# LayerNorm statistics joined on GpSimd in an attention and ternary feed-forward layer

## The chip, the cores and the metric

The kernel runs on one core of a Trainium2 chip. The time is the device time of one execution in microseconds (us); the time before is the median of three runs. The engines are called as the profile calls them: PE (TensorE matrix products; PEld its weight loads), DVE (VectorE), ACT (ScalarE), POOL (GpSimd) and SP (SyncE, which only issues DMAs here).

## The reference, cut to what matters

The input x has 8 batches of 1024 tokens with 256 features. Four LayerNorms over the 256 features stand in the layer:

```python
x = x + layernorm(attention(layernorm(x), Wq, Wk, Wv, Wo))
x = x + layernorm(ternary_ffn(layernorm(x), weight, alpha, bias))

def layernorm(x, eps=1e-05):
    m = mean(x, axis=-1); v = var(x, axis=-1)
    return (x - m) / sqrt(v + eps)
```

The attention has 16 heads of 16 features on 4 key and value heads, with rotary positions, softmax over 1024 keys, and an output product. The feed-forward part is one 256x256 product with weights in {-1, 0, 1}, scaled by alpha, plus a bias.

## The kernel before

**Units and blocks.** The work is cut into 16 units of 512 tokens (four tiles of 128 tokens on the 128 partitions; two units are one batch). Each unit has four blocks of attention, one for each of four groups of heads: 64 blocks, each some 25 us long. In a block PE makes the scores twice: once with queries on the partitions (tile sm, L600), from which DVE takes the maxima of the rows (mx, L625), and once with keys on the partitions, shifted by those maxima (se, L673), from which ACT takes the exponentials (e, L694). PE then sums them with the values (av, L714). The maxima go back into the stacked queries through PE (L648), ACT (L650), DVE (ml, L657) and two DMAs by SP (L664). Each block's maxima are made ahead of its exponentials.

**What runs between the blocks.** Class Project makes a later unit's queries, keys and values: LayerNorm of x in two halves p = 0 and 1 (begin: statistics, xn, its split into a high and a low part xs), transposes pt_xt, products, rotation of the queries (rotate, L315 to L317) and of the keys (kt), their split (split, L157 and L162, tiles hlq and ks), and stores to DRAM (dq, dk), from where DMAs stack them into q_st and k_st. Class Tail takes an earlier unit's attention output to the end: fetch and scale, the output product pa (attn), stats_a with x1 = x + layernorm, stats_x with the second LayerNorm xn and its split hl, transposes pt_ot (x, L267), the feed-forward product (ffn, with the bias added on POOL at L853), stats_f and the output (end). Tables such as P_PARTS and T_PARTS give the step of the schedule at which each part stands; there are 32 steps to a unit. Unit 0's tail and the first projects have tables of their own (T_FIRST, P_FIRST, P_SECOND). Units 12 to 14 use another form of the tail, which transposes xn itself (xw).

**Order.** PE's, DVE's and ACT's instructions run in the order in which the program writes them. POOL's do so only at the start and in the last unit's end; in the long middle part the framework's scheduler chooses POOL's order, and SP's, from its own estimates:

```python
with tc.manual_schedule(engines={E.PE, E.DVE, E.Activation}):
    while s < 4 * NSTEP:
        s = window(s)
```

Each engine works its own queue in order and waits for the others by semaphores.

**Statistics.** ln_stats (L231 to L244) makes bn_stats for each of one or two tiles on DVE (L237; six numbers for each token: count, mean and sum of squared deviations of the even columns, and the same of the odd ones), then bn_aggr on DVE (L239; mean and variance, tile mv), then three small steps on POOL: variance plus epsilon (L241), the power -0.5 (L242) and the negative mean (L243), into tile lnsc. ln_apply (L253) uses them on POOL, or on DVE for parts of the start and of the last unit. There are 134 calls: eight at the start (units 0, 1 and 2), 26 in the projects from unit 3 on, 90 in the tails of units 0 to 14, and twelve in the last unit's, which go one tile at a time, the first tile on POOL and the other three on DVE. The small tiles have four buffers each.

Of the kernel before, what the change touches and what calls it, by code (L numbers as in the profile page):

```python
# [8 lines left out]
F32 = mybir.dt.float32  # L9
F32R = mybir.dt.float32r  # L10
AF = mybir.ActivationFunctionType
ALU = mybir.AluOpType
# [4 lines left out]
P = 128  # L17
# [6 lines left out]
EPS = 1e-5  # L24
# [4 lines left out]
def kernel(  # L29
# [29 lines left out]
    nc = tc.nc  # L59
    B, S, D = x.shape  # L60
# [14 lines left out]
    small = ctx.enter_context(tc.tile_pool(name="small", bufs=4))  # L75
# [10 lines left out]
    def load_x(u, tag, bufs):  # L86
        b, half = divmod(u, UPB)
        t = xp.tile([P, UT, D], F32, tag=tag, name=f"{tag}_{u}", bufs=bufs)
        src = x[b, half * UQ : (half + 1) * UQ, :].rearrange("(t p) d -> p t d", p=P)
        for ts in (slice(0, 2), slice(2, 4)) if u == 0 else (slice(0, 4),):  # L90
            nc.sync.dma_start(out=t[:, ts, :], in_=src[:, ts, :])
        return t

    x_sb = {0: load_x(0, "x", 2)}
# [4 lines left out]
    mhalf = const.tile([P, 2], F32, name="mhalf")  # L99
# [128 lines left out]
        nc.scalar.copy(wt, pt)  # L228


    def ln_stats(src):  # L231

        n = src.shape[1]
        mv = small.tile([P, 2, 2], F32, tag="mv", name="mv")[:, :n]
        st = small.tile([P, 2, 6], F32, tag="bnst", name="bnst")
        for t in range(n):
            nc.vector.bn_stats(st[:, t, :], src[:, t, :])  # L237
        for t in range(n):
            nc.vector.bn_aggr(mv[:, t, :], st[:, t, :])  # L239
        sc = small.tile([P, 2, 2], F32, tag="lnsc", name="lnsc")[:, :, :n]  # L240
        nc.gpsimd.tensor_scalar(sc[:, 1, :], mv[:, :, 1], EPS, 1.0, ALU.add, ALU.mult)  # L241
        nc.gpsimd.tensor_tensor(sc[:, 1, :], sc[:, 1, :], mhalf[:, :n], ALU.pow)  # L242
        nc.gpsimd.tensor_scalar(sc[:, 0, :], mv[:, :, 0], -1.0, 0.0, ALU.mult, ALU.add)  # L243
        return mv, sc  # L244

    def ln_apply(eng, dst, src, stats):
        mv, sc = stats
        for t in range(src.shape[1]):
            if eng is nc.scalar:
                eng.activation(dst[:, t, :], src[:, t, :], AF.Identity, bias=sc[:, 0, t : t + 1])  # L250
                eng.mul(dst[:, t, :], dst[:, t, :], sc[:, 1, t : t + 1])
                continue
            eng.tensor_scalar(  # L253
                dst[:, t, :],
                src[:, t, :],
                sc[:, 0, t : t + 1] if eng is nc.gpsimd else mv[:, t, 0:1],
                sc[:, 1, t : t + 1],
                ALU.add if eng is nc.gpsimd else ALU.subtract,
                ALU.mult,
            )  # L260
# [62 lines left out]
    class Project:  # L323
# [19 lines left out]
                    for p in range(2)  # L343
                ]

        def stats(self, p):
            self.sc[p] = ln_stats(x_sb[self.u][:, 2 * p : 2 * p + 2, :])

        def norm(self, p, eng=None):
            src = x_sb[self.u][:, 2 * p : 2 * p + 2, :]  # L350
# [6 lines left out]
            split_lo(eng or self.eng, self.xs[p][1], self.xn[p], self.xs[p][0])  # L357

        def begin(self, p):
            self.stats(p)  # L360
            self.norm(p)
            self.hi(p)
            self.lo(p)
# [374 lines left out]
    class Tail:  # L738
# [88 lines left out]
            ln_apply(self.eng(p), self.on[p], self.x1[p], self.sc[p])  # L827

        def stats_a(self, p):
            self.sc[p] = ln_stats(self.a[p])  # L830
            self.add(p)

        def stats_x(self, p):
            self.sc[p] = ln_stats(self.x1[p])
            self.norm(p)
            if not NU - 4 <= self.u < NU - 1:
                self.split(p)

        def stats_f(self, p):
            self.sc[p] = ln_stats(self.a[p])  # L840
            self.end(p)

        def ffn(self, p):
# [482 lines left out]
```

## Time and profile before

| What | Value |
|---|---|
| Median of three runs | 1629.83 us (1627.93 to 1637.51) |
| The profiled execution | 1631.22 us, span 1629.4 us, mean granted PE clock 0.993 |
| Busy PE / DVE / ACT / POOL | 1578.1 / 1398.3 / 1270.4 / 833.2 us |
| bn_aggr on DVE, two-tile and one-tile calls (L239) | 256 instructions, 38.6 us |
| Power on POOL, 128x2 (L242) | 122 instructions, 85.7 us |
| Idle POOL ahead of L241 | 337.8 us in all |

The profile is of one execution. Busy is the time in which an engine works on an instruction; the span runs from the first to the last instruction, and the execution's own time is some 1.8 us longer. A group of instructions is told by line, engine, operation, tiles written and read with their shapes, and count; then busy time in us, mean ns of one, and the idle time of the engine just before them with what ended most of it. A line of a timeline has start and duration in us, engine, line, operation and tiles, and in brackets the idle time before it. "x2" after it means two such instructions in a row.

### The profile page before, as it was taken

The numbers are of one execution on the slowest core, as the hardware profiler recorded it, in microseconds if no ns is written. First come the engines' busy times: TensorE is split into PE (matmuls) and PEld (weight loads), VectorE is DVE, ScalarE is ACT, GpSimd is POOL, SyncE is SP. The second block draws the span as 40 slices with busy tenths as digits, with TensorE's granted clock in tenths as the row PEclk, the third lists the DMA queues.
The fourth block names the chain that finished last, engine by engine and source line by source line (L and its number), as shares of the span: only waits on it lengthen the run. The fifth ranks groups of instructions, "written<-read, shape, count | busy, mean of one in ns | idle before, by whom it ended". The sixth has DMA issues, their size and how long they took to land.

```text
span 1629.4 us, 37176 instructions
## 1 busy us (share of the span) xinstructions
PE 1578.1 (97%) x14698; PEld 816.7 (50%) x14698; DVE 1398.3 (86%) x2050; ACT 1270.4 (78%) x2473; POOL 833.2 (51%) x1239
## 2 busy tenths in 40 slices
PE   7999999999999999999999999999999999999997
PEld 5544454554545545454544545455454554444444
DVE  7878888889898888989889898988989888999964
ACT  4667878788787887878788787887878787787784
POOL 5542357374654647455364845546474552333354
PEclk8999999999999999999999999999999999999999
DMA  4151516124141422514133161413314151131100
GB/s 140 53 83 49 106 53 113 62 67 112 57 108 47 88 71 60 125 47 104 61 79 80 57 128 38 103 56 82 80 57 97 47 105 46 43 74 34 42 15 27
DMA packets 86078, 117.98 MB, mean 72 GB/s; under 512 B 12088, under 2 KB 50808, under 8 KB 85752
## 3 DMA queue, kind: packets, MB, share of 16 engines
q1 hardware_dynamic: 85904, 115.60, 29.7%
q8 instruction: 116, 1.90, 0.5%
q14 instruction: 58, 0.48, 0.1%
HBM read 68.65 MB, written 45.88 MB: 70 GB/s over the span
## 4 chain that ended last, share of the span: by engine, by line
PE 81%; DVE 10%; POOL 3%; ACT 2%; issue 1%; DMA 1%; SPq 0%; POOLq 0%; ACTq 0%; DVEq 0%
PE av L714 29%; PE se L673 28%; PE sm L600 9%; DVE mx L625 8%; PE pa L301 3%; PE pq L301 3%; PE pf L301 2%; ACT e L694 2%; PE pt_xt L267 2%; PE pt_ot L267 1%; PE pkv L301 1%; PE pm L648 1%; DVE bnst L237 1%; POOL lnsc L242 0%; POOL xn L253 0%
## 5 line engine op out<-in xcount | busy, mean ns | idle before, releaser
L625 DVE TENSOR_REDUCE mx<-sm 128x2 f32<-128x1024 f32 (+1 forms) x1305 | 1205.1, 972 | 184.4 <-PE sm L600 164.7
L694 ACT ACTIVATE e<-se 128x512 f32<-128x512 f32 x1996 | 1056.9, 603 | 221.6 <-PE sm L600 176.2
L600 PE MATMUL sm<-k_st,q_st 64*128 64x512 f32 x2048 | 747.3, 449 | 7.9 <-DVE mx L625 4.6
L673 PE MATMUL se<-q_st,k_st 64*128 64x512 f32 x2048 | 705.9, 441 | 17.1 <-ACT e L694 14.6
L714 PE MATMUL av<-e,v_aug 128*32 128x256 f32 (+3 forms) x8600 | 605.7, 378 | 0.0
L673 PEld LDWEIGHTS se<-q_st,k_st 64*128 64x128 f32 x2048 | 325.1, 185 | 392.6 <-ACT e L694 303.6
L600 PEld LDWEIGHTS sm<-k_st,q_st 64*128 64x128 f32 x2048 | 325.7, 185 | 68.8 <-DVE mx L625 46.0
L714 PEld LDWEIGHTS av<-e,v_aug 128*32 128x32 f32 x8600 | 193.9, 109 | 213.0 <-issue 148.7
L241 POOL TENSOR_SCALAR lnsc<-mv 128x2 f32<-128x2 f32 (+1 forms) x134 | 25.6, 191 | 337.8 <-DVE mv L239 331.2
L788 POOL TENSOR_TENSOR xn<-xn,a 128x512 f32<-128x512 f32 x30 | 38.4, 1281 | 130.0 <-DMA a<-d_rec 104.5
L242 POOL TENSOR_TENSOR lnsc<-lnsc,mhalf 128x2 f32<-128x2 f32 (+1 forms) x134 | 92.2, 689 | 0.9
L157 POOL TENSOR_SCALAR xs<-xn 128x512 fp32r<-128x512 f32 x27 | 17.1, 634 | 128.3 <-DMA dq<-hlq 127.0
L162 POOL TENSOR_TENSOR hl<-xn,hl 128x512 fp32r<-128x512 f32 x54 | 68.7, 1284 | 0.1
L853 POOL TENSOR_TENSOR a<-a,bias_bc 128x512 f32<-128x512 f32 x30 | 38.4, 1280 | 53.7 <-ACT a L852 53.7
L253 POOL TENSOR_SCALAR xn<-x,lnsc 128x256 f32<-128x256 f32 x116 | 64.2, 560 | 2.3
L301 PE MATMUL pa<-woh,hl 128*128 128x256 f32 x240 | 46.2, 295 | 1.1 <-ACT e L694 1.1
L315 POOL TENSOR_TENSOR t<-q_rot,sin_q_sb 128x512 f32<-128x512 f32 x31 | 39.6, 1279 | 12.8 <-ACT q_rot L457 12.7
L237 DVE BATCH_NORM_STATS2 bnst<-x 128x6 f32<-128x256 f32 x124 | 45.9, 412 | 0.0
L301 PE MATMUL pq<-xt,wqkvh 128*128 128x256 f32 x256 | 45.0, 299 | 0.5 <-ACT e L694 0.5
L237 DVE BATCH_NORM_STATS2 bnst<-a 128x6 f32<-128x256 f32 x120 | 44.5, 413 | 0.1
L162 POOL TENSOR_TENSOR hlq<-q_rot,hlq 128x512 fp32r<-128x512 f32 x31 | 39.8, 1284 | 4.8 <-ACT hlq L159 4.5
L457 ACT COPY q_rot<-pq 128x512 f32<-128x512 f32 x32 | 18.7, 585 | 29.5 <-PE pq L301 29.5
(164 smaller groups left out, 1329.7 us busy)
## 6 DMA issues: line engine op xcount, KB each, us to landing
q_st<-dq SPq DMA_DIRECT2D x90, 256.0 KB
dq<-hlq SPq DMA_DIRECT2D x60, 256.0 KB
d_av<-avsb SPq DMA_DIRECT2D x60, 256.0 KB
x<-in_L_attn_x SPq DMA_DIRECT2D x15, 512.0 KB
xn<-d_av SPq DMA_DIRECT2D x30, 256.0 KB
a<-d_rec SPq DMA_DIRECT2D x30, 256.0 KB
xr<-in_L_attn_x SPq DMA_DIRECT2D x15, 512.0 KB
out_x<-a SPq DMA_DIRECT2D x30, 256.0 KB
```

Of the source, the lines that this page charges most:

```text
L162: eng.tensor_tensor(lo, src, hi.bitcast(F32), ALU.subtract)
L237: nc.vector.bn_stats(st[:, t, :], src[:, t, :])
L242: nc.gpsimd.tensor_tensor(sc[:, 1, :], sc[:, 1, :], mhalf[:, :n], ALU.pow)
L253: eng.tensor_scalar(dst[:, t, :], src[:, t, :], sc[:, 0, t : t + 1] if eng is nc.gpsimd else mv[:, t, 0:1], sc[:, 1, t : t + 1], ALU.add i ...
L267: nc.tensor.transpose(pt[:, c, t * P : (t + 1) * P], src[:, t, c * P : (c + 1) * P], ident_r)
L301: nc.tensor.matmul(out, chunk(left[i], c), chunk(right[j], c), start=(k == 0), stop=(k == len(steps) - 1),)
L315: eng.tensor_tensor(dst, x, table.unsqueeze(1).to_broadcast(list(x.shape)), ALU.mult)
L600: scores = nc.tensor.matmul(sm[0][:, part, :], queries[rows], k_st[(u // UPB) % 3][rows, r2, ch * 512 : (ch + 1) * 512], start=True, stop= ...
L625: early[0] = nc.vector.tensor_reduce(mx[i][:, a, head_and_tile(i, r2, t), lo:n], sm[0][:, lo:n, :], AX.X, ALU.max).ins
L673: nc.tensor.matmul(sc if len(queries.shape) == 2 else sc.rearrange("p (j t) -> p j t", j=G), k_st[(i // G // UPB) % 3][rows, r2, kt * P : ...
L694: nc.scalar.activation(e, sc, AF.Exp, scale=1.0 / D**0.5)
L714: nc.tensor.matmul(av_ps[0][32 * r : 32 * r + 32, lo:hi], va[:, kt, r, :], es[i * NK + kt, r // 2, r % 2][:, lo:hi], start=(kt == 0 and lo ...
```

## The change

A function join_stats is added. Where ln_stats is called with joined_by = nc.gpsimd, DVE makes only bn_stats, and POOL makes mean and variance out of the halves itself, for one or two tiles at once: the negative mean is -0.5 times the sum of the two means; the sums of squares are added and divided by 256, with epsilon; the square of (even mean + negative mean) is added; then comes the power. That is five tensor_tensor, two tensor_scalar and the power, eight instructions in place of POOL's three and DVE's one or two bn_aggr. It holds for the projects' begin (units 3 to 15) and for every tail part whose engine is POOL: units 0 to 14, and the first tile of the last unit. The statistics of units 0 to 2 at the start and of the last unit's other tiles stay as they were.

```diff
-    def ln_stats(src):
+    def join_stats(neg_mean, rstd, st):
+
+        eng, (m0, m1), (s0, s1) = nc.gpsimd, (st[:, 1, i] for i in range(2)), (
+            st[:, 2, i] for i in range(2)
+        )
+        eng.tensor_tensor(neg_mean, m0, m1, ALU.add)
+        eng.tensor_scalar(neg_mean, neg_mean, -0.5, 0.0, ALU.mult, ALU.add)
+        eng.tensor_tensor(s0, s0, s1, ALU.add)
+        eng.tensor_scalar(s0, s0, 1.0 / D, EPS, ALU.mult, ALU.add)
+        eng.tensor_tensor(m0, m0, neg_mean, ALU.add)
+        eng.tensor_tensor(m0, m0, m0, ALU.mult)
+        eng.tensor_tensor(rstd, s0, m0, ALU.add)
+        eng.tensor_tensor(rstd, rstd, mhalf[:, : rstd.shape[1]], ALU.pow)
+
+    def ln_stats(src, joined_by=None):
 
         n = src.shape[1]
-        mv = small.tile([P, 2, 2], F32, tag="mv", name="mv")[:, :n]
         st = small.tile([P, 2, 6], F32, tag="bnst", name="bnst")
         for t in range(n):
             nc.vector.bn_stats(st[:, t, :], src[:, t, :])
+        sc = small.tile([P, 2, 2], F32, tag="lnsc", name="lnsc")[:, :, :n]
+        if joined_by is nc.gpsimd:
+            join_stats(sc[:, 0, :], sc[:, 1, :], st[:, :n].rearrange("p t (i k) -> p k i t", i=2))
+            return None, sc
+        mv = small.tile([P, 2, 2], F32, tag="mv", name="mv")[:, :n]
         for t in range(n):
             nc.vector.bn_aggr(mv[:, t, :], st[:, t, :])
-        sc = small.tile([P, 2, 2], F32, tag="lnsc", name="lnsc")[:, :, :n]
...
-        def stats(self, p):
-            self.sc[p] = ln_stats(x_sb[self.u][:, 2 * p : 2 * p + 2, :])
+        def stats(self, p, joined_by=None):
+            self.sc[p] = ln_stats(x_sb[self.u][:, 2 * p : 2 * p + 2, :], joined_by)
...
         def begin(self, p):
-            self.stats(p)
+            self.stats(p, nc.gpsimd)
...
         def stats_a(self, p):
-            self.sc[p] = ln_stats(self.a[p])
+            self.sc[p] = ln_stats(self.a[p], self.eng(p))
...
         def stats_x(self, p):
-            self.sc[p] = ln_stats(self.x1[p])
+            self.sc[p] = ln_stats(self.x1[p], self.eng(p))
...
         def stats_f(self, p):
-            self.sc[p] = ln_stats(self.a[p])
+            self.sc[p] = ln_stats(self.a[p], self.eng(p))
```

## The prediction

> **What bounds the kernel now.** I read the page first, then the busy time by stages, the chain of work that ended last, the groups of instructions by shape, and the timelines of POOL and PE around the first unit's tail.
>
> ```profile
> PE 1578.1 (97%) x14698; PEld 816.7 (50%) x14698; DVE 1398.3 (86%) x2050; ACT 1270.4 (78%) x2473; POOL 833.2 (51%) x1239
> ...
> PE 81%; DVE 10%; POOL 3%; ACT 2%; issue 1%; DMA 1%; SPq 0%; POOLq 0%; ACTq 0%; DVEq 0%
> ```
>
> PE is busy 97% of the span and carries 81% of the chain; DVE carries 10%. So a shorter DVE pays only in the places where DVE is on that chain. By stages (columns: PE, PEld, DVE, ACT and POOL busy with their counts, PE clock, DMA share, GB/s):
>
> ```profile
> 200.00:300.00 100.00, 97.81 (x954) 50.82 (x954) 86.57 (x131) 79.30 (x154) 56.79 (x82) 1.00 0.39 89
> 900.00:1000.00 100.00, 98.51 (x958) 51.22 (x952) 88.49 (x130) 80.86 (x158) 54.19 (x80) 1.00 0.33 78
> 1400.00:1500.00 100.00, 97.84 (x930) 46.73 (x928) 91.68 (x132) 80.36 (x157) 34.56 (x53) 1.00 0.26 56
> ```
>
> Up to about 1300 us PE hardly pauses. There the chain by stretches of 100 us gives DVE 3.6% (the score maxima alone, no statistics). From 1300 us on, where no projections are left, DVE rises to 14 to 23% of it.
>
> **What is removed from DVE.** 119 of the 134 statistics lose their bn_aggr: 116 with two tiles and 3 with one, 235 instructions. PE's, ACT's and DVE's order is written by hand and otherwise stays.
>
> ```profile
> L239 DVE BATCH_NORM_AGGREGATE mv<-bnst 128x2 f32<-128x6 f32 x256 | 38.6, 173 | 0.4
> L241 POOL TENSOR_SCALAR lnsc<-mv 128x2 f32<-128x2 f32 x122 | 23.3, 191 | 318.5 <-DVE mv L239 312.4
> L242 POOL TENSOR_TENSOR lnsc<-lnsc,mhalf 128x2 f32<-128x2 f32 x122 | 85.7, 702 | 0.5
> L316 POOL TENSOR_TENSOR q_rot<-q_rot,t 128x256 f32<-128x256 f32 x31 | 23.1, 745 | 0.5
> L316 POOL TENSOR_TENSOR k_rot<-k_rot,t2k 128x128 f32<-128x128 f32 x14 | 6.4, 457 | 1.0
> ```
>
> 235 x 0.173 = 40.7 us less DVE work. On the chain stand only nine pairs or singles of L239 between 1300 and 1580 us, eight with 0.22 and one with 0.18 us (the pairs overlap with their neighbours): **-1.9 us**. Its bounds are 0 and all 16 statistics of that stretch at 2 x 0.173, -5.5 us.
>
> **What is added to POOL.** A join is eight instructions, two tensor_scalar, five small tensor_tensor and the power, in place of two tensor_scalar and the power. A two-column tensor_tensor without a power isn't in the trace. From the rows with 256 and 128 columns, (745 - 457) / 128 = 2.25 ns a column, so two columns end near 0.17 us; I take 0.19, the tensor_scalar's row. The lower bound is 0.10 (the 128x2 memset of L100 took 99 ns), the upper one 0.70, the power, which is the same instruction in the same shape. 119 x 5 x 0.19 = 113 us more POOL work, 833 to 946 of 1629: still far from full, so only queueing counts. A statistic alone in an idle POOL is ready 0.95 us later, less the 0.35 that DVE gives back.
>
> [...] The row first: L241 to L243 starts 0.27 us apart where its span is 0.19. [...]
>
> **Steady units (1 to 11).** PE first needs POOL's result in the transposes pt_ot of the tail. The trace has the first half of hl ready 3.7 to 5.3 us before its transpose for p = 0 (unit 1: written 343.77, used 347.52) and 5.6 us or more before for p = 1. POOL's queue isn't ordered by hand after the start. In the built kernel the join's steps stand between the query's rotation and split, and the low half of that split (1.28 us) now goes ahead of hl. So hl is late by 1.28 + 0.95 = 2.2 us, some 2.5 with waits: inside every slack. x1 is 0.7 us late where DVE comes 8 us after. The next unit's x is waited for by POOL itself behind a DMA of 11 to 13 us. I cost eleven units at nothing; the cover is those 3.7 us.
>
> **Unit 0, where the cover is thin.** Its tail runs while unit 4's keys and queries are rotated and split, and POOL has a backlog from 232 us on:
>
> ```profile
> 231.93 0.74 POOL L315 TENSOR_TENSOR t2k<-k_rot,sin_kt_sb 128x256 f32<-128x256 f32 x1 [1.79 <-DMA k_rot<-d_k]
> ...
> 248.02 1.09 POOL L253 TENSOR_SCALAR xn<-x,lnsc 128x256 f32<-128x256 f32 x2
> 249.08 1.28 POOL L315 TENSOR_TENSOR t<-q_rot,sin_q_sb 128x512 f32<-128x512 f32 x1
> 250.32 0.63 POOL L157 TENSOR_SCALAR hl<-xn 128x512 fp32r<-128x512 f32 x1
> 250.91 1.29 POOL L315 TENSOR_TENSOR q_rot<-q_rot,cos_q_sb 128x512 f32<-128x512 f32 x1
> 251.76 0.53 PE L267 MATMUL pt_ot<-ident_r,hl 128*128 128x128 f32 x4
> 252.14 1.29 POOL L162 TENSOR_TENSOR hl<-xn,hl 128x512 fp32r<-128x512 f32 x1
> ```
>
> hl's first half ends at 250.95, PE uses it at 251.76: slack 0.81. Between t2k and that instruction the built kernel's queue holds more:
> - Moved ahead of it: the rest of the second half of the query, cos 1.29, subtract 0.74, add 0.75, split 0.62 and 1.29 = 4.7 us.
> - First statistic (its three steps were done before): two small steps and the power, 2 x 0.19 + 0.70 = 1.1.
> - Second and third: five small steps more each, 1.9.
> - Fourth (x1 of p = 1; nothing of it stood ahead before): five, 0.95.
>
> Together 8.6 us: hl ends near 259.6, and PE, in order, stands **7.8 us**. Fifteen of the steps are tensor_tensor, so with 0.10 each it is 15 x 0.09 = 1.3 less, 6.5, and with 0.70 it is 15 x 0.51 = 7.7 more, 15.5. Behind the transposes PE holds all scores and values, ACT its exponentials and DVE its maxima; as PE is the bound, nothing is given back. On SP's queue the stack of block 7's maxima (L664, issued at 241.67 and 242.41 before) now goes behind key loads k_st that wait for dk to land. Its second half I put near 245.6 issued and 247.6 landed, where PE took that block up at 244.93; but this wait of some 2.5 us lies ahead of the same transpose and is part of the 7.8, as POOL needs nothing from PE in between. The fetch of unit 1 that is moved behind hlq's stores is used at 301 us, 40 us on.
>
> A standing PE loses clock (columns as above):
>
> ```profile
> 104.00:108.00 4.00, 3.00 (x16) 1.15 (x16) 3.45 (x5) 1.19 (x3) 0.00 (x0) 0.78 0.35 74
> 108.00:112.00 4.00, 4.00 (x36) 2.06 (x36) 2.49 (x3) 2.79 (x6) 0.00 (x0) 0.79 0.00 0
> ```
>
> After one microsecond of idle PE the clock was 0.78 and 0.79 for 8 us: 0.215 x 8 = **1.7 us** (bounds 0, and twice it, 3.4, if it drops for both waits).
>
> **The end.** Unit 14's xn was written at 1572.19 and transposed at 1572.52: 0.3 of slack against 0.95 to 1.6 us more, **+1.3**. From 1585.5 us on the chain goes through POOL's lnsc steps themselves: two joins are on it (unit 14's outputs, at 1586.32 and 1600.71), +0.95 each, less the step L242 of the last unit that moves ahead of an addition of 1.28 us, and less three DVE pairs of 0.22 us ahead of them: 1.9 - 1.3 - 0.7 = 0, **+0.4** with five waits of 0.08 inside a chain. Bounds for both together: 0, and at 0.70 a step 3 x 5 x 0.51 = 7.7 more, 9.4.
>
> **The sum.** +7.8 + 1.7 + 1.3 + 0.4 - 1.9 = **+9.3 us**. The profiled execution took 1631.22 us (span 1629.4, some 1.8 around it) and would become 1640.5. It lies 1.4 above the median of three runs, 1629.83; on that the forecast is **1639.1 us**, +0.6%. About 1% is what a measurement of this kernel can tell from no change, so this counts as the same.
>
> [...] The row: POOL's 128x512 tensor_tensor took 1.27 to 1.34 us in the first stage, with DVE busy 75%, and 1.28 in the one with 92%, so no contention shows. [...]
>
> **Rivals.**
> - *Slower by over 1%: the small steps are dear.* A two-column tensor_tensor costs what the power does, 0.70. For it: it is the only tensor_tensor of this shape that the trace has. Against: its one-column form takes 0.55, so work by the column is in it, the 128-column row without a power takes 0.46, and the tensor_scalar 0.19. Then unit 0 costs 15.5, the clock 1.7, the end 9.4, and in steady units hl is late by 1.28 + 5 x 0.70 = 4.8, which is 1.1, 1.1 and 0.6 us over the slack in the three units that have 3.7, 3.7 and 4.2 (2.8): 15.5 + 1.7 + 9.4 + 2.8 - 1.9 = +27.5, **1657.3 us**. It decides from some 0.43 a step, where 30 x 0.24 = 7 us more bring +9.3 to 1%.
> - *Faster: DVE paces PE everywhere.* DVE is 88% busy, and every aggregation taken away shortens a round: -40.7 + 9.5 + 1.7 = -29.5, **1600.3 us**. Against: the chain has nine of 235 on it, and DVE waited 102 us for PE's sm between 300 and 1300 us, PE's loads 19 for DVE.
> - *The thin place doesn't hold PE:* POOL's backlog is worked off sooner than its rows add up, or PE has other work there. Then 1.7 at the end against -1.9: **1629.6 us**. Against: PE's order is fixed.
>
> **How the numbers follow.** Forecast 0.60, dear steps 0.18, DVE as the pace 0.07, no wait 0.15. The predicted time is the forecast's. The range, 1628 to 1650, goes from the no-wait case with a little more DVE relief up to dear steps of half that price; the forecast's own is 1633 to 1645. Faster by over 1% is the DVE case, 0.07. Slower by over 1% (above 1646.1) is 0.18 and 0.04 of the forecast's upper tail; the rest is the same, 0.71.
>
> **What would show it.** Right: DVE's busy time down by some 40 us; POOL's up by some 110; the new small steps near 0.19 us; one PE wait of 6 to 9 us between 244 and 262 us released by POOL hl L157 or by the maxima's DMA, with a clock below 1 after it; the same stretches of 100 us between 300 and 1300 us with PE busy 98%, just shifted. Wrong: pt_ot waits for POOL in every unit (dear steps), units shorter than before (DVE's pace), or no wait at 250 us.

## The result, and the profile after

The changed kernel took a median of 1640.43 us (1637.69 to 1649.57 in eight runs) against 1629.76 for the kernel before in the same rounds: a ratio of 1.0068, 95% interval [1.0049, 1.0087]. The profiled execution took 1639.94 us (span 1638.2) where that of before took 1631.22 (span 1629.4): +8.7, where the sum forecast +9.3; by the medians of the same rounds it is +10.7. The time is inside the forecast's own range. The loss is clear of the noise, as the interval leaves out 1, but at 0.7% it is "the same" by the bound of 1%. The total hides errors in its terms, which the experiments below bring out.

The page of the changed kernel, busy engines and the chain's shares by engine:

```profile
PE 1576.4 (96%) x14698; PEld 815.4 (50%) x14698; DVE 1375.4 (84%) x1815; ACT 1270.1 (78%) x2473; POOL 938.4 (57%) x1834
...
PE 73%; DVE 10%; POOL 9%; DMA 3%; ACT 2%; issue 2%; SPq 0%; POOLq 0%; ACTq 0%
```

POOL has 105 us more work and 9% of the chain instead of 3. DVE's union of busy time fell by only 22.9 us, though 235 instructions are gone: two bn_aggr in a row overlap each other and the instruction behind them (0.173 us each by their row, but a pair at 481.40 us of the kernel before ends after 0.30 us and the next instruction starts after 0.23).

The busy time by stages (PE, PEld, DVE, ACT, POOL with counts, PE clock, DMA share, GB/s):

```profile
200.00:300.00 100.00, 91.57 (x885) 47.94 (x884) 77.40 (x105) 72.80 (x141) 60.54 (x119) 0.97 0.34 78
900.00:1000.00 100.00, 98.52 (x959) 51.02 (x957) 87.38 (x113) 81.02 (x158) 60.40 (x119) 1.00 0.32 76
1400.00:1500.00 100.00, 97.95 (x946) 47.33 (x948) 90.72 (x117) 80.42 (x158) 38.48 (x82) 1.00 0.24 53
```

Between 200 and 300 us PE lost 6.2 us of busy time and some of its clock. The other two stretches look as before.

The groups of the statistics by shape:

```profile
L236 POOL TENSOR_TENSOR lnsc<-bnst 128x2 f32<-128x2 f32 x116 | 22.7, 195 | 229.0 <-DVE bnst L250 229.0
L240 POOL TENSOR_TENSOR bnst<-bnst,lnsc 128x2 f32<-128x2 f32 x116 | 22.4, 193 | 7.3
L243 POOL TENSOR_TENSOR lnsc<-lnsc,mhalf 128x2 f32<-128x2 f32 x116 | 81.3, 701 | 8.8
L257 DVE BATCH_NORM_AGGREGATE mv<-bnst 128x2 f32<-128x6 f32 x21 | 3.4, 176 | 0.2
```

The new small tensor_tensor takes 0.192 to 0.197 us over its five rows, two of which are shown, as the row of the tensor_scalar had promised; the dear-steps rival is out. (The 21 bn_aggr left at L257 are two for each of the start's six calls, which the section on the kernel before counts as eight, and the last unit's nine: 6 + 26 + 90 + 12 make the 134.)

Unit 0's tail on POOL, from the first rotation of unit 4's keys to hl:

```profile
230.86 0.73 POOL L332 TENSOR_TENSOR t2k<-k_rot,sin_kt_sb 128x256 f32<-128x256 f32 x1 [2.08 <-DMA k_rot<-d_k]
...
249.44 0.20 POOL L240 TENSOR_TENSOR bnst<-bnst,lnsc 128x2 f32<-128x2 f32 x1
249.59 1.28 POOL L332 TENSOR_TENSOR q_rot<-q_rot,cos_q_sb 128x512 f32<-128x512 f32 x1
250.82 0.20 POOL L241 TENSOR_TENSOR bnst<-bnst 128x2 f32<-128x2 f32 x1
250.97 0.73 POOL L333 TENSOR_TENSOR q_rot<-q_rot,t 128x256 f32<-128x256 f32 x1
...
255.84 1.09 POOL L270 TENSOR_SCALAR xn<-x,lnsc 128x256 f32<-128x256 f32 x2
256.90 0.19 POOL L240 TENSOR_TENSOR bnst<-bnst,lnsc 128x2 f32<-128x2 f32 x1
257.06 0.62 POOL L157 TENSOR_SCALAR hl<-xn 128x512 fp32r<-128x512 f32 x1
```

And what PE waited for there:

```profile
244.04 0.47 PE L690 MATMUL se<-q_st,k_st 64*128 64x512 f32 x1 [0.20 <-DMA q_st<-ml]
246.24 0.46 PE L690 MATMUL se<-q_st,k_st 64*128 64x512 f32 x1 [1.47 <-DMA q_st<-ml]
257.73 0.75 PE L284 MATMUL pt_ot<-ident_r,hl 128*128 128x128 f32 x4 [4.95 <-POOL hl L157]
```

From the start of t2k to the end of hl's first half it is 26.8 us now (257.68 - 230.86) and was 19.0 (250.95 - 231.93). PE waits 6.6 us in three pieces, 1.7 of them for the maxima's DMA. The small steps are worked between the long ones: many steps of the joins wait in POOL's queue behind a piece of the query's rotation or split.

PE's clock in the same place (columns as above):

```profile
244.00:248.00 4.00, 2.49 (x18) 1.37 (x20) 1.92 (x2) 1.68 (x3) 3.92 (x8) 0.91 0.17 39
248.00:252.00 4.00, 4.00 (x30) 1.44 (x26) 3.56 (x5) 3.52 (x7) 3.92 (x7) 0.66 0.54 192
252.00:256.00 4.00, 0.78 (x4) 0.37 (x4) 2.03 (x4) 1.30 (x3) 3.84 (x10) 1.00 0.20 38
256.00:260.00 4.00, 2.27 (x22) 1.31 (x22) 0.00 (x0) 0.58 (x1) 3.91 (x8) 0.69 0.46 146
260.00:264.00 4.00, 4.00 (x40) 2.23 (x42) 3.25 (x6) 2.97 (x6) 3.47 (x7) 0.88 0.42 147
```

It fell after both waits. Busy time by what was missing: 2.49 x 0.09 + 4 x 0.34 + 2.27 x 0.31 + 4 x 0.12 = 2.8 us.

**A ruler for small effects.** The copy avsb by ACT ends each of the first 63 of the 64 blocks (counted from 0; the last one ends in smaller copies). The end of the same block in two profiles, subtracted, shows where the time went with a resolution of about 0.1 us, far below the spread of whole runs. In us, against the profile of the kernel before (whose own times are in the first line; a falling number is a gain):

| Kernel | 221.5 | 321.5 | 1261.1 | 1566.8 | end 1629.4 |
|---|---|---|---|---|---|
| changed kernel | -1.07 | 8.05 | 6.09 | 4.55 | 8.72 |
| e1_no_unit0 | -0.50 | -0.70 | -3.10 | -4.64 | -0.51 |
| e2_no_end | -2.12 | 8.52 | 5.94 | 4.57 | 4.12 |
| e3_neither | -1.24 | -1.44 | -4.00 | -5.37 | -6.25 |
| e4_only_unit0 | -1.36 | 7.64 | 7.74 | 7.74 | 6.93 |
| e6_even | -3.38 | -4.02 | -6.37 | -7.94 | -9.48 |
| e7_hl_first | -0.97 | 0.97 | -0.78 | -0.96 | 3.59 |
| e8_no_last | 0.41 | 8.74 | 6.60 | 5.03 | 7.37 |
| e11_second_half | -0.71 | -0.86 | -3.25 | -3.25 | -4.13 |

Four things happen to the changed kernel: +9.1 between 221 and 321 us (unit 0's tail), then a slow gain of 2.0 up to 1261 us (the drift), another of 1.5 up to 1567 us, and +4.2 at the end. The first column differs between any two profiles, mostly by PE's clock near 105 us (1.7 us in the kernel before, told at the end) and by when the start is done: the same matmul stands at 103.63 us in e6_even and at 107.15 in e8_no_last.

### The profile page after: what moved, and what is told of

It reads as the page before. It is cut to its first block, busy times and chain, and to the rows that moved or that the text cites. A ratio compares the mean times of both kernels' runs of the same rounds, so it can differ in the third digit from the quotient of the medians.

```text
span 1638.2 us, 37522 instructions
## 1 busy us (share of the span) xinstructions
PE 1576.4 (96%) x14698; PEld 815.4 (50%) x14698; DVE 1375.4 (84%) x1815; ACT 1270.1 (78%) x2473; POOL 938.4 (57%) x1834
## 4 chain that ended last, share of the span: by engine, by line
PE 73%; DVE 10%; POOL 9%; DMA 3%; ACT 2%; issue 2%; SPq 0%; POOLq 0%; ACTq 0%
PE av L731 26%; PE se L690 25%; PE sm L617 9%; DVE mx L642 8%; PE pa L318 3%; PE pq L318 2%; PE pf L318 2%; ACT e L711 2%; PE pt_xt L284 2%; PE pkv L318 1%; PE pt_ot L284 1%; POOL hl L162 1%; PE pm L665 1%; POOL hlq L162 1%; DVE bnst L250 1%
## 5 line engine op out<-in xcount | busy, mean ns | idle before, releaser
L236 POOL TENSOR_TENSOR lnsc<-bnst 128x2 f32<-128x2 f32 (+1 forms) x119 | 23.2, 195 | 232.1 <-DVE bnst L250 232.1
L243 POOL TENSOR_TENSOR lnsc<-lnsc,mhalf 128x2 f32<-128x2 f32 (+1 forms) x119 | 83.0, 698 | 8.9
```

Source lines behind the costliest of these rows:

```text
L243: eng.tensor_tensor(rstd, rstd, mhalf[:, : rstd.shape[1]], ALU.pow)
```

## The experiments

In each, "joiner" is a method added to the tail that says whether a statistic is joined on POOL; the three calls of ln_stats use it in place of self.eng(p).

**Unit 0's tail undone.**

```diff
+        def joiner(self, p):
+            return self.eng(p) if self.u > 0 else None
...
-            self.sc[p] = ln_stats(self.a[p], self.eng(p))
+            self.sc[p] = ln_stats(self.a[p], self.joiner(p))
```

> Only unit 0's tail keeps bn_aggr (6 of the 119 joins are undone); all others are joined on POOL. POOL's order between the keys' rotation of unit 4 and hl of unit 0 is then that of the kernel before.
> Theory 1 (the loss is unit 0's wait for POOL, +9.1 with its clock, and the end, +4.2, against small gains of 3.5 in between): the 6.6 us of PE waits between 244 and 258 us go, and so does the clock below 0.9 there; the time falls by 8 to 9.5 us against the changed kernel and comes to +0 to +2 against the kernel before. The blocks' ends stand within 0.5 us of the kernel before up to block 9 and drift to about -2 at block 50.
> Rival A (each of 119 joins costs a little, 10.2 / 119 = 0.09 us): six joins less give -0.5, the time stays at +9 to +10 against before.
> Rival B (the order of SP's queue, the maxima behind the key loads, is the cause, not POOL): the wait before q_st<-ml stays if SP's order stays; some 2 to 3 us of it remain.

Measured: 1630.37 us against 1630.63, ratio 0.9997 [0.9981, 1.0012]. The transposes of unit 0 in this kernel:

```profile
251.25 0.54 PE L284 MATMUL pt_ot<-ident_r,hl 128*128 128x128 f32 x4
```

No bracket: no wait, nor one for q_st<-ml before it, and no loss between 221 and 321 us. Six joins of 119 made the whole loss of 9 us. Rival A (a price for every join) falls. Rival B (SP's order) can't be told apart here, as SP's queue is back in the order of before too; e7_hl_first below does that. What the kernel gains later (-3.9 to 1567 us) it loses again at the end.

**The end undone.** As above, with `self.u < NU - 2`.

> The tails of units 14 and 15 keep bn_aggr (7 joins undone), all others are joined on POOL.
> Theory 1: unit 0 loses the same 8 to 9.5 us at 244 to 262 us, the drift of -3.5 up to 1566 us stays, and the last 70 us cost nothing more than before (the shift at the end of the span equals that of block 61, within 1 us, where the changed kernel loses another 4.2). Time 3 to 5 us below the changed kernel, +4.5 to +7 against before.
> Rival A (0.09 us for each join): -0.6 against the changed kernel, +9 to +10 against before.

Measured: 1635.22 us, ratio 1.0026 [1.0015, 1.0038], +4.6 us. Unit 0 loses again (10.6 us by the table), the last column is 4.12 after 4.57: nothing is lost at the end. (Nine joins are undone, six of unit 14 and three of unit 15, not the seven that the expectation counts; the next kernel has 104, not 106.)

**Both undone.** With `0 < self.u < NU - 2`.

> The tails of unit 0 and of units 14 and 15 keep bn_aggr; the other 106 joins (tails of units 1 to 13, projects of units 3 to 15) are on POOL.
> Theory 1: no PE wait in unit 0, nothing lost at the end, the drift of -0.24 us a unit and of -1.5 between 1310 and 1566 us stays: -2 to -5 us against before, faster than both kernels.
> Rival A: 106 x 0.09 = +9 against before.
> Rival C (the drift was chance between two profiles): -1.5 to 0.

Measured: 1625.68 us, ratio 0.998 [0.9964, 0.9995], about -3 us by the ratio and -5 by the medians. 104 of the 119 joins together are a small gain. This version beats both kernels. The drift is there again (-2.6 from 321 to 1261 us), so it is no chance between two profiles, and rival C falls.

**Unit 0 alone.** Only `self.u == 0` joins, and the projects' begin keeps bn_aggr.

> Only the six statistics of unit 0's tail are joined on POOL; all others keep bn_aggr.
> Theory 1: the whole loss of unit 0 with six joins: PE waits 6 to 7 us between 244 and 258 us, clock 0.65 to 0.9 there, blocks from 9 on late by 8 to 9.5 us against before. After that no drift, if the drift is DVE's relief in the steady units (shift of block 61 as that of block 9 within 0.5 us), and nothing at the end: +8 to +9.5 against before.
> Rival A (0.09 us a join): +0.5.
> Rival C (the backlog needs the projects' joins too, which stand ahead of unit 0's): the wait is 1 us or more shorter than in the changed kernel.

Measured: 1638.57 us, ratio 1.0058 [1.0045, 1.007], +7.9 us. Its row in the table is flat from 321 to 1567 us: with bn_aggr in the steady units the drift is gone. Its waits:

```profile
245.91 0.47 PE L690 MATMUL se<-q_st,k_st 64*128 64x512 f32 x1 [1.47 <-DMA q_st<-ml]
257.47 0.75 PE L284 MATMUL pt_ot<-ident_r,hl 128*128 128x128 f32 x4 [5.82 <-POOL hl L157]
```

The wait isn't shorter than in the changed kernel (7.3 us in place of 6.6): the projects' joins play no part in it, and rival C falls.

**The steps kept, the long work held back.** One small copy makes the second half of unit 4's query wait for hl:

```diff
             t2 = work.tile([P, 2, 2 * P], F32, tag="t2", name=f"t2_{self.u}_{p}", bufs=1)
+            if self.u == 4 and p == 1:
+                first = tails[0].hl[0][:, 0, 0, 0:1].bitcast(F32)
+                nc.gpsimd.tensor_scalar(t2[:, 0, 0:1], first, 1.0, 0.0, ALU.mult, ALU.add)
             rotate(eng, rot, cos_q_sb[:, ts], sin_q_sb[:, ts], t2)
```

> As the changed kernel, with one POOL step more: one column of hl of unit 0 (p = 0) is copied into the scratch tile of the second half of unit 4's query, before it is rotated. So that half (six instructions, 5.7 us by their starts) can no longer go ahead of hl, and the steps of the joins stay.
> Theory 1 (the moved work, not the steps, makes the wait): from the start of t2k hl is ready after 20.7 us, where the kernel before has 19.0 and the changed one 26.8; PE waits 0 to 0.5 us for it, the wait for q_st<-ml (1.5 to 2.2 us) stays with a clock loss of 0 to 1.7. 4.5 to 7 us less than the changed kernel, +3 to +6 against before.
> Rival D (the added steps themselves fill POOL, the order is secondary): the wait falls by less than 2 us, the time stays at +7 or more.

Measured: 1633.53 us against 1629.93, ratio 1.0022 [1.001, 1.0034], +3.6 us where the changed kernel has +10.7. POOL around hl:

```profile
230.98 0.74 POOL L332 TENSOR_TENSOR t2k<-k_rot,sin_kt_sb 128x256 f32<-128x256 f32 x1 [2.10 <-DMA k_rot<-d_k]
...
249.94 1.10 POOL L270 TENSOR_SCALAR xn<-x,lnsc 128x256 f32<-128x256 f32 x2
251.12 0.62 POOL L157 TENSOR_SCALAR hl<-xn 128x512 fp32r<-128x512 f32 x1
251.82 1.27 POOL L162 TENSOR_TENSOR hl<-xn,hl 128x512 fp32r<-128x512 f32 x1
253.08 0.18 POOL L486 TENSOR_SCALAR t<-hl 128x1 f32<-128x1 f32 x1
```

hl is ready 20.8 us after t2k's start, as expected, and PE's wait for its first half is gone (0.69 us are left for the second half, at 264.87). Unit 0 costs 1.9 us in place of 9.1. The copy holds back a little more than the change had moved: the product with sin (1.24 us by its starts) stood ahead of hl in the kernel before too. With it there, the steps alone would make hl some 3.0 us late, an estimate from these starts, and that is 2.2 over the slack. So the joins' own time on POOL is the smaller part; what hurt more is that the scheduler lets other long work go ahead of what the eighth step releases. That it does so because the eight steps wait for each other is likely, but not shown.

The 1.5 us for q_st<-ml stay, because SP keeps the order of the changed kernel: the two halves are issued at 241.87 and 244.22 us with key loads between them, where the kernel before issues them in a row from 241.67. This is rival B's share: 3.0 us by the end of block 6 (249.0 us in the profile before), with the clock behind it. Rival B falls only as the whole cause. In this profile another 1.2 us were lost at 1552 us, where the clock fell to 0.76 after waits of 0.46 and 0.45 us; no other kernel here shows that, and its reason is open.

**The last unit's first tile undone.** With `self.u < NU - 1`.

> Only the last unit's first tile keeps bn_aggr (3 joins undone); unit 14 is joined.
> Theory 1: the end's 4.2 us are unit 14's xn: PE waits 2.2 us in the transposes pt_ot at 1579 us, with a clock of 0.75 to 0.85 for 8 us after it (1.7 us). So the loss between block 61 and block 62 stays at 3 to 4 us, and at most 1 us of it goes.
> Rival E (the last unit's chain of small steps): the span loses 3 to 4 us against the changed kernel.

Measured in one run: 1638.59 us. The expectation failed: the end costs 2.3 us (5.03 to 7.37) in place of 4.2, and 1.1 of them in the block after 1567 us in place of 3.2. Rival E's 3 to 4 us did not come either; 1.8 of the end's loss are gone. POOL of the changed kernel shows why:

```profile
1572.09 0.19 POOL L236 TENSOR_TENSOR lnsc<-bnst 128x1 f32<-128x1 f32 x1 [2.35 <-DVE bnst L250]
...
1573.74 0.56 POOL L243 TENSOR_TENSOR lnsc<-lnsc,mhalf 128x1 f32<-128x1 f32 x1
1574.42 0.55 POOL L270 TENSOR_SCALAR v_aug<-v_aug,lnsc 128x256 f32<-128x256 f32 x1
1574.93 0.19 POOL L236 TENSOR_TENSOR lnsc<-bnst 128x2 f32<-128x2 f32 x1
...
1577.28 0.70 POOL L243 TENSOR_TENSOR lnsc<-lnsc,mhalf 128x2 f32<-128x2 f32 x1
...
1578.26 1.09 POOL L270 TENSOR_SCALAR xn<-x,lnsc 128x256 f32<-128x256 f32 x2
```

In the hand-written order of the end, the last unit's first statistic (128x1) stands ahead of unit 14's (128x2), and POOL works both joins one after the other before xn. PE's transposes behind them, in the changed kernel and in e8_no_last:

```profile
1578.87 1.23 PE L296 MATMUL pt_ot<-ident,xn 128*128 128x128 f32 x4 [2.20 <-POOL xn L270]
```

```profile
1578.34 0.98 PE L296 MATMUL pt_ot<-ident,xn 128*128 128x128 f32 x4 [0.99 <-POOL xn L270]
```

The clock behind it, changed kernel first, then e8_no_last (columns as above):

```profile
1576.00:1580.00 4.00, 1.63 (x6) 0.76 (x6) 1.32 (x5) 1.80 (x4) 3.52 (x14) 0.81 0.00 0
1580.00:1584.00 4.00, 4.00 (x38) 1.54 (x37) 0.00 (x0) 1.63 (x4) 3.76 (x13) 0.76 0.02 4
```

```profile
1576.00:1580.00 4.00, 2.27 (x28) 1.17 (x30) 2.16 (x6) 2.76 (x5) 3.41 (x12) 1.00 0.02 4
1580.00:1584.00 4.00, 3.66 (x31) 1.15 (x24) 0.34 (x1) 2.72 (x7) 3.82 (x10) 1.00 0.00 0
```

With one join the wait is half as long and the clock keeps at 1.00; with two it falls, which costs another 1.63 x 0.19 + 4 x 0.24 = 1.3 us. In e1_no_unit0, with both joins, the wait is 2.23 us and the four transposes take 1.23 us as in the changed kernel, against 0.98 here; that the clock stays at 1.00 with one join rests on one profile.

**DVE's relief alone.** Neither bn_aggr nor joining; POOL's three old steps take the even columns' numbers, so that the odd columns are left out of these statistics:

```diff
-            join_stats(sc[:, 0, :], sc[:, 1, :], st[:, :n].rearrange("p t (i k) -> p k i t", i=2))
+            nc.gpsimd.tensor_scalar(sc[:, 1, :], st[:, :n, 2], 2.0 / D, EPS, ALU.mult, ALU.add)
+            nc.gpsimd.tensor_tensor(sc[:, 1, :], sc[:, 1, :], mhalf[:, :n], ALU.pow)
+            nc.gpsimd.tensor_scalar(sc[:, 0, :], st[:, :n, 1], -1.0, 0.0, ALU.mult, ALU.add)
```

> DVE's relief alone: neither bn_aggr nor the joining steps. POOL's three old steps read mean and sum of squares of the even columns straight from bn_stats' output; the odd columns are left out of these 119 statistics. POOL has the work of the kernel before, DVE 235 bn_aggr less.
> Theory 1 (with what the first four runs added: the relief counts only where a pair of bn_aggr stands in the chain of maxima, one pair of 0.24 us a unit and more of them after 1310 us): no wait in unit 0, -0.25 us a unit, -1.2 to -1.6 between 1310 and 1566 us; -4 to -7 us against before.
> Rival B (DVE sets PE's pace, and POOL's added work hides it): all 40.7 us come out, near 1590 us.

Measured: 1625.11 us against 1629.93, ratio 0.9971 [0.9959, 0.9982]. The drift is that of the joined kernels, -2.35 from 321 to 1261 us and -1.57 to 1567. Even with nothing added to POOL the 235 aggregations are worth about 5 us, not 40: DVE doesn't set the pace.

**One statistic of each unit.** Joins only in the second half of the projects (13 statistics):

```diff
-            self.stats(p, nc.gpsimd)
+            self.stats(p, nc.gpsimd if p == 1 else None)
```

with the three calls in the tails left without a joiner.

> The kernel before, with a join for nothing but the second half (p = 1) of the projects of units 3 to 15: 13 statistics, 26 bn_aggr of 235. It is the one statistic of a steady unit after which DVE goes straight on to the maxima that PE waits for.
> Theory 1: the blocks' ends lose 0.24 us in each unit, -2 to -2.5 at block 50 against block 9, as with all 119 joins, and nothing in unit 0, after 1310 us or at the end: -2 to -3.5 us against before.
> Rival F (every aggregation taken away gives a little, 2.0 / 180 = 0.01 us each): -0.3 at most.

Measured: 1627.65 us, ratio 0.999 [0.9972, 1.0007], which alone can't tell it from nothing. The ruler can: -0.86 at 321 us, -3.25 at 1261, and flat after it. So 26 of the 235 aggregations hold the whole gain of the steady units, and the tails' joins that of 1310 to 1567 us. DVE at that place in the kernel before, and in this one:

```profile
480.75 0.74 DVE L237 BATCH_NORM_STATS2 bnst<-x 128x6 f32<-128x256 f32 x2
481.40 0.30 DVE L239 BATCH_NORM_AGGREGATE mv<-bnst 128x2 f32<-128x6 f32 x2
481.63 0.34 DVE L657 SCALAR_TENSOR_TENSOR ml<-mh,low,pm 32x128 fp32r<-32x128 f32 x1
481.89 3.53 DVE L625 TENSOR_REDUCE mx<-sm 128x2 f32<-128x1024 f32 x4
```

```profile
479.63 0.74 DVE L250 BATCH_NORM_STATS2 bnst<-x 128x6 f32<-128x256 f32 x2
480.29 0.32 DVE L674 SCALAR_TENSOR_TENSOR ml<-mh,low,pm 32x128 fp32r<-32x128 f32 x1
480.54 1.80 DVE L642 TENSOR_REDUCE mx<-sm 128x2 f32<-128x1024 f32 x2
```

Without the pair, ml follows the statistics after 0.66 us instead of 0.88; the shift of 0.22 runs through the maxima behind it into PE's next products.

**How thick the cover of the steady units is.** Four, and in a second kernel ten, further small steps between the power and xn in the tails of units 1 to 11:

```diff
             self.sc[p] = ln_stats(self.x1[p], self.eng(p))
+            if 0 < self.u < 12:
+                for _ in range(4):
+                    rstd = self.sc[p][1][:, 1, :]
+                    nc.gpsimd.tensor_scalar(rstd, rstd, 1.0, 0.0, ALU.mult, ALU.add)
             self.norm(p)
```

> The changed kernel with four more small steps (tensor_scalar 128x2, each waiting for the one before) between the power and xn in the second LayerNorm of the tails of units 1 to 11: 88 steps. POOL's order stays as in the changed kernel.
> Theory 1 (steady units are covered): hl is 4 x 0.27 = 1.1 us later; in the changed kernel its first half lies 2.4 to 3.0 us ahead of its transpose. So nothing: the blocks' ends up to block 50 within 0.5 us of the changed kernel, the time within 1 us of it, +8 to +11 against before.
> Rival A (POOL's added work costs as such): 88 steps in place of the change's 595 and for the same price each, 10.2 x 88 / 595 = +1.5 us against the changed kernel; if hl has no slack, 11 units x 1.1 = +12.

Measured: 1639.38 us, ratio 1.0071 [1.0046, 1.0096], the changed kernel's. In its profile, which was slower from the start, the blocks stand 8.60 us behind the changed kernel's at 123 us and 8.23 at 1267: four steps more ahead of each half's hl, and nothing lost. The cover is thin by then: PE waits for hl twice between 300 and 1300 us, 0.8 and 0.5 us.

> The same with ten steps, 220 in all. Besides the steps' own 2.7 us, POOL's order moves the next query half's product with sin (1.25 us) and parts of the next joins ahead of hl.
> Theory 1: hl's first half is 4 us later or more, its second half some 6, over slacks of 2.4 to 3.5 us: PE waits 1 to 3 us for POOL in the first transposes pt_ot of each of the eleven units, more where the second half of the tail is late as well, and the clock falls below 1 after it. +20 to +60 us against the changed kernel.
> Rival A (each added step costs the same, wherever it stands): 10.2 x 220 / 595 = +3.8 us.

Measured: 1711.97 us, ratio 1.0509 [1.0484, 1.0534], +82.6 against before and so some +72 against the changed kernel, more than expected. By the blocks of its profile it is 3.0 us ahead of the changed kernel at 330 us and 66.6 behind at 1363: some 6 us a unit. PE's waits from 300 to 1300 us (total, times, longest):

```profile
PE pt_ot L284 <- POOL hl L157: 44.9, 20, 3.2
PE pt_ot L284 <- POOL hl L162: 7.3, 7, 1.1
```

Four steps more for a statistic cost nothing, ten cost 6 us a unit: it is a threshold, not a price for each step. The ten don't act alone. As expected POOL's order moved too: in unit 1 the product with sin (1.27 us) and two steps of the next join now stand ahead of hl's first half, and behind four steps they did not. The expectation priced one wait a unit; most units wait twice, once for each half of the tail.

## Why the prediction was right or wrong, step by step

**The mechanism was right in unit 0.** This one place where POOL's result is waited for makes the larger loss, 9 us, and the end the rest; e1_no_unit0 and e4_only_unit0 show unit 0's from both sides. Its pieces:

- *hl late by 8.6 us.* Measured 7.8 from t2k's start. Of these the moved work is 4.4 by its starts (cos 1.23, subtract and add 0.69 each, split 0.58 and 1.25; forecast 4.7), and 3.4 are left for the small steps (forecast 3.9). They were taken a little too dear: less the power's 0.68, the 17 others take 2.7 us by their starts, 0.16 each and not 0.19, because after many of them the next instruction starts 0.15 us later (249.44 to 249.59), after others 0.27.
- *PE's wait 7.8.* Measured 6.6 in the changed kernel and 7.3 in e4_only_unit0, 7.8 - 0.8 of slack. The q_st<-ml part, "some 2.5 us", was 1.7 and lay inside, as forecast.
- *The clock 1.7.* 2.8 by the rows: it fell after both waits, which stood as the upper bound. In e4_only_unit0 it fell after the second alone (0.50 from 256 to 260 us), so this term has luck in it. Together 9.4 by pieces and 9.1 by the ruler, against 9.5 forecast.

**The steady units at nothing: half right.** Their cover held: four more steps cost nothing, and the transposes pt_ot lost 4.9 us between 300 and 1300 us in both kernels. But the gain there was put at 0, and it is 2.0 us over some ten units of the changed kernel, 0.24 a unit in e11_second_half. The step that failed is the reading of the chain up to 1300 us as "the score maxima alone, no statistics". The chain names the instruction that ended last at each point; the pair of bn_aggr stood ahead of ml and maxima on DVE's in-order queue and delayed them without being named. It is not the rival of DVE's pace either: one pair in eight counts (e11_second_half), the rest of the relief is idle time.

**DVE's relief after 1300 us: -1.9.** Measured -1.5 by the ruler (-1.6 in e6_even). That no contention of POOL with DVE shows holds after the change too: the gain is there, and POOL's 128x512 tensor_tensor for hl has a mean of 1.281 us after and 1.284 before.

**DVE's busy time, -40.7.** It fell by 22.9. The rows were added by their means although a pair takes 0.23 us by starts (481.40 to 481.63), not 2 x 0.173. In e11_second_half 13 pairs less are 2.9 us, 0.22 a pair.

**The end: +1.7.** Measured +4.2, the worst term in proportion. The step "0.3 of slack against 0.95 to 1.6 us more" counted one join and some waiting; two stand in series there, of which the first belongs to another unit (e8_no_last). And the clock after that wait, 1.3 us, was priced in unit 0 but not here. The +0.4 for the chain through lnsc behind it is +0.9 by the ruler (7.79 at block 62 to 8.72).

So the sum came out because 2.5 us too little at the end stood against 2.0 of gain not seen in the steady units and 1.1 by which this profile's start was faster. The right total is no proof of the terms.

## What to carry to other kernels

Moving work to an engine with room is decided by what its longer chain is queued with, not by the added busy time: of 105 us more work on POOL nearly all was free in units 1 to 13, and the few joins in unit 0 cost 9 us, where a scheduler filled the gaps of an eight-step chain with long work that nobody waited for yet. Look for the tight places first, keep the old form there (here 15 calls of 119), and give the new form the rest. And read a relief of a well-filled engine by where the instruction stands in its in-order queue: one pair of bn_aggr in eight stood ahead of something that PE waits for, though the chain of waits never named it.

## What the runs showed of the hardware

**The same wait cost nothing in nine profiles and 8 us in one.** Near 105 us each of the twelve profiles has a PE wait of 0.99 to 1.00 us for a maximum, in code that no version changes. After it nine of them, the changed kernel's too, kept the clock at 1.00; that of before had 0.78 and 0.79 in two stretches of 4 us, e4_only_unit0 0.68 and 0.89, and e10_four_steps half speed for some 20 us. These are means: in the kernel before the single microseconds from 106 to 110 us have 0.62, 0.50, 0.50 and 0.67 and those around them 1.00, so it is half speed for some 3.4 us (the 0.38, 0.50, 0.50 and 0.33 that are missing make 1.7), and that fall takes 1.7 us. The rows of the changed kernel and of e10_four_steps right after it:

```profile
108.00:112.00 4.00, 4.00 (x42) 2.18 (x41) 3.28 (x4) 2.73 (x7) 0.00 (x0) 1.00 0.00 0
```

```profile
108.00:112.00 4.00, 4.00 (x23) 2.19 (x22) 2.07 (x3) 2.12 (x4) 0.00 (x0) 0.50 0.02 6
```

In the latter the profile lost 8.4 us against the changed one within one block, as much as the whole effect studied here. Several kernels have single runs some 7 to 11 us above their median (1637 to 1641 of the kernel before); the only one with a profile is this of e10_four_steps, 1648.0 against a median of 1639.38, so for the others this cause is likely, not shown. What decides whether the clock falls after that wait is not shown.

**A small POOL step cost 0.15 or 0.27 us, not its span.** The span is 0.19 to 0.20. After a small tensor_tensor the next instruction starts 0.15 us later where it doesn't need the result (L236 to L238) and 0.27 where it does (L242 to L243). Need alone is not the rule: after the tensor_scalar L239 it is 0.25 to 0.28 us also in the 22 cases where the next instruction is a piece of the keys' split (11) or of a query's rotation (11) that needs nothing of it, and from L241 to L243 of the kernel before, which don't need each other, it is 0.27; the reason is open.
